# Second attention with stored values: one and three projection steps in turn, the output projection, the maxima and the next layernorm in other places

## The chip, the cores and the metric

One core of one Trainium2 chip. The metric is device microseconds of one execution; of several runs the median is told. Five engines work at once, each on its own queue in order: PE (TensorE matmuls; PEld is its weight load), DVE (VectorE), ACT (ScalarE), POOL (GpSimd) and SP (SyncE, which here issues nearly all DMA transfers). They wait for each other through semaphores.

## The reference

Four layers on a batch of 32 sequences of 128 tokens with 256 features, all in float32, each added to its input after a layernorm. The change touches the end of layer 2 and layer 3.

```python
x = x + _L0_xattn_ref(_layernorm(x), ctx_1024, ctx_1024, mask)      # 16 heads of 16, no weights
x = x + _L0_ffn_ref(_layernorm(x), w_gate, w_up, w_down)            # quantised, 256 -> 768 -> 256
x = x + _L1_xattn_ref(_layernorm(x), ctx_1024, ctx_1024, Wq, bq, ...)
x = x + _L1_ffn_ref(_layernorm(x), W1, b1, W2, b2, Wr, br)          # 8 experts, the best one per token

# _L1_xattn_ref: 16 heads of 64
q = query @ Wq + bq; k = key @ Wk + bk; v = value @ Wv + bv
attn = softmax(q k^T / 8)                                           # per head
out = (attn v) @ Wo + bo + residual
return (out - mean) * rsqrt(var + EPS) * ln_gamma + ln_beta
```

The quantised FFN rounds its activations with scales that are maxima over the whole batch, so its parts are separated by a global maximum each.

## The kernel before

The layers run one after the other. The order on PE, DVE, ACT and POOL is the order of the program text (`manual_schedule(engines=by_hand)`); SP is not in that set, and a planner places its transfers among each other.

**The FFN's last quantisation (about 465 to 543 us).** A loop over 16 half tiles (`order`, line 778 on) multiplies the quantised gate by the quantised up projection on ACT (L793, L796) and DVE (L799, L574). PE is free there, so the values of layer 3 are projected beside it: for 20 of the 32 sequences (`NF * G`) `project_v` multiplies the turned context tile `cf` by `wv_f` into PSUM (6 buffers), `take_v` copies the result to `vs` (5 buffers) on ACT or DVE, and SP stores it to `v_d` in DRAM. `load_v(b)` loads `cf` from DRAM; its pool `vf` has 2 buffers. Line 783 asks for the tile of block 4 + s once block 2 + s is projected. The first four halves (sequences 0 and 1) are projected in the stage before. When the loop is done, the global maximum `amax_o` gives `s_o` and `k_o` (L812 to L817), and the down projection begins with `quant_o` (L1195 on DVE, L1197 on ACT).

**The second attention (652 to 1290 us).** Two sequences are a group (`G`), 16 groups in all. A unit `n` is half the heads of one sequence `b`: 8 heads, `hf` is the half; a group has 4 units, `u` is the unit's place in it. Unit n does the following.

- `scores_c(n + 1)` on PE into the PSUM tiles `sc0` and `sc1` (one buffer each), `maxima(n + 1)` on DVE (L1012), `exps(n + 1, 0)` and `(n + 1, 1)` on ACT (L1021, 4 heads each, into `pr`, with sums), `normal_c(n + 1)`, which divides half on DVE and half on POOL (L1030, L1033).
- `transpose_c(n)` turns `pr` on PE into two `pt_p` tiles (2 buffers, shared with `pt_n`) and copies them to `prT` on ACT (L1048); `values_c(n)` multiplies by v (L1059) and copies to `oT` on ACT (L1066).
- Steps of the next group's projections: `step(g + 1, k)` for k = 0 to 7 computes 128 columns of K and of Q into one PSUM tile (L950; tag mm, 2 buffers), which its `take` copies to kT on ACT (L956) and to qT on DVE (L960). The rows of Q come from `rT`, the turned layernorm of the group.
- For an earlier sequence: `project_o` (L1072, 16 matmul instructions), `finish_1` to `finish_4` (sum, layernorm, residual, next layernorm, store of the row to `rows_d` by SP), `turn` and `logits` (PE, with the copy xnT on ACT), `route` (DVE: the best expert), `count` (PE, into the spare part of the `pt_n` tile) and `place` (DVE, then a scatter by POOL).
- For group g + 2: `norm_stats` (DVE, a power on POOL), `norm_apply` (DVE, two sums on POOL), `turn_group` and `turned_group` (PE, DVE: rT), and for group g + 3 `load_c` (three transfers on SP).

Where the next group's v comes from DRAM (`g + 1 < NF`, groups 0 to 8, 36 units) a unit has two steps: the short branch, which the change rewrites. Otherwise (28 units) three, since v has to be projected there; this branch is not rewritten.

Of the kernel before, what the change touches and what calls it, by code (L numbers as in the profile page):

```python
# [8 lines left out]
F32 = mybir.dt.float32  # L9
# [11 lines left out]
P = 128  # L21
# [15 lines left out]
def tile_xattn_ffn_d2(  # L37
# [27 lines left out]
    KD = D // P  # L65
# [588 lines left out]

    def load_v(b):
        if b < NF * G:
            cfs[b] = vf.tile([P, KD, P], F32, tag="cf", name="cf")
            nc.sync.dma_start(out=cfs[b], in_=ct_d[b])

    def project_v(b, h, ps):  # L660
# [9 lines left out]
        copy(vs, ps)  # L670
        nc.sync.dma_start(out=v_d[b, :, h * 512 : (h + 1) * 512], in_=vs)

    load_v(0)
    load_v(1)
    with (
        tc.tile_pool(name="bel", bufs=2, side="left") as el,
        tc.tile_pool(name="b_mu", bufs=6, space=PSUM) as pmm,
# [42 lines left out]
        for t in range(NT):  # L720
            up(t, 0)
            quant_g(t, 0)
            up(t, 1)
            sigmoid(t, 0)
            up(t, 2)
            if t % 2:
                b, h = divmod(t // 2, 2)
                ps_v = pv.tile([P, 512], F32, tag="v", name="ps_vf")
                project_v(b, h, ps_v)
                take_v(b, h, ps_v, el, nc.scalar.copy)  # L730
                if h:
                    load_v(b + 2)
            quant_s(t, 0)
            quant_g(t, 1)
            gate(t, 0)
            absmax("u", t, 0, ups[t, 0])
            up(t, 3)
            sigmoid(t, 1)
            up(t, 4)
            quant_s(t, 1)  # L740
            up(t, 5)
            if t < NT - 1:
                gate(t, 1)
            absmax("u", t, 1, ups[t, 1])
# [8 lines left out]
    with (  # L753
# [27 lines left out]
        for s, n in enumerate(order):  # L781
            took, taken = taken, []
            for h in range(2):
                taken.append(pv.tile([P, 512], F32, tag="v", name="ps_vf"))
                project_v(2 + s, h, taken[h])
            load_v(4 + s)
            if s >= KEPT:
                load_u(s + FU - 1)
            t, i = divmod(n, 2)
            r = half(gates[t], i)  # L790
            u = ups[t, i]
            u16 = ql.tile([P, HM, TB], I16, tag="u16", name="u16")
            nc.scalar.activation(u16, u, AF.Copy, scale=i_u)  # L793
            take(s, 0)
            gs16 = ql.tile([P, HM, TB], I16, tag="gs16", name="gs16")
            nc.scalar.activation(gs16, r, AF.Copy, scale=k_s)  # L796
            take(s, 1)

            nc.vector.scalar_tensor_tensor(r, gs16, s_s, u16, ALU.mult, ALU.mult)  # L799
            absmax("o", t, i, r)  # L800
# [296 lines left out]
    def finish_3(b):  # L1097
        t = tiles[b]
        t["ln"] = stats([t["row"][:, :D]], 1, "e")
# [228 lines left out]
    with tc.manual_schedule(engines=by_hand):  # L1328
        norm_stats(1)
        norm_apply(1)  # L1330
        values_of(0)
        for n in range(M1):
            step(0, n)()
# [10 lines left out]
        for n in range(N):  # L1344
            b, hf = divmod(n, 2)
            g, u = divmod(n, 2 * G)
            if u == 0 and g + 1 < NG:
                values_of(g + 1)
            nf = 2 if g + 1 < NF else 3
            fill = [  # L1350
                (lambda k=nf * u + j: step(g + 1, k)) if g + 1 < NG and j < nf
                else (lambda n=3 * (u if g + 1 == NG else -1) + j: others(n))
                for j in range(3)
            ]
            done = b - 2 if hf == 0 and b > 1 else None
            more = n + 1 < N
            if nf == 3:
                if more:
                    scores_c(n + 1)
                if u == 0 and g + 1 < NG and "rT" not in groups_[g + 1]:  # L1360
# [37 lines left out]
            else:  # L1398

                scores_c(n + 1)  # L1400
                maxima(n + 1)
                if hf and b > 0:
                    finish_1(b - 1)
                if u == 3:
                    norm_apply(g + 2)
                    load_c(g + 3)
                if done is not None:
                    finish_4(done)
                takes = [fill[0]()]
                exps(n + 1, 0)  # L1410
                transpose_c(n)
                takes.append(fill[1]())
                takes[0]()
                exps(n + 1, 1)
                takes[1]()
                if hf and b > 0:
                    finish_2(b - 1)
                values_c(n)
                if done is not None:
                    turn(done)  # L1420
                normal_c(n + 1)
                if u == 3:
                    turn_group(g + 2)
                    turned_group(g + 2)
                if hf and b > 0:
                    finish_3(b - 1)
                if hf == 0 and b > 0:
                    project_o(b - 1)
                if done is not None:
                    logits(done)  # L1430
                    if done > 0:
                        count(done - 1, tiles[done]["spare"])
                    route(done)
                    if done > 0:
                        place(done - 1)
            if u == 0 and g + 2 < NG:
                norm_stats(g + 2)
            if u == 2 and nf == 3 and g + 2 < NG:
                norm_apply(g + 2)
                if g + 3 < NG:  # L1440
                    load_c(g + 3)
            if u == 3 and nf == 3 and g + 2 < NG:
                turn_group(g + 2)
            if n == 8:
                first_weights()
# [301 lines left out]
```

## Time and profile before

| | us |
|---|---|
| median of 3 runs | 1617.8 (1615.79 to 1618.09) |
| the profiled execution | 1616.39 |
| its span | 1614.7 |
| values projected, last quantisation | 464.9 to 543.4 |
| down projection of the FFN | to 633.4 |
| short units of the second attention | 652.0 to 994.1 |
| its other units | 994.1 to 1290 |
| experts | 1330 to 1614.7 |
| PE busy in the span | 1521.8 |
| DVE / ACT / POOL busy | 950.5 / 809.0 / 461.1 |
| granted TensorE clock, mean | 0.988 |

The span runs from the first to the last instruction; the execution's time is 1.7 us longer. In a line of instructions in order of time stand the start, the length, the engine, the line of the program, the operation, output and inputs, the shape and the number of instructions that were merged; brackets tell how long the engine stood idle before it and who ended that. Matmul ends are modelled, so the distance from one start to the next tells more than the lengths.

### The profile page before, as it was taken

Reading aid. Unit: us, or ns where it says so; the run is one execution under the profiler, and the core shown is the slowest. Engines: PE = TensorE matmul, PEld = TensorE weight load, DVE = VectorE, ACT = ScalarE, POOL = GpSimd, SP = SyncE. Lnnn points to the kernel's source line nnn. Section 1 sums busy time; section 2 is a strip of 40 time slices with the busy share of each in tenths; the row PEclk is TensorE's granted clock in tenths of the full one; section 3 lists DMA queues with packets and bytes.
Section 4 is the critical chain, followed back from the end, with each engine's and each line's share of the span. In section 5 each row is a group of like instructions: output and inputs, shape, how many; then the busy total and the mean of one; then the engine's idle time right before and its main releaser. Section 6 shows DMA issues by size and latency. Waiting matters only on the chain. (4 is left out here: it accounts for less than half of the span.)

```text
span 1614.7 us, 28238 instructions
## 1 busy us (share of the span) xinstructions
PE 1521.8 (94%) x10062; PEld 1132.9 (70%) x10062; DVE 950.5 (59%) x2275; ACT 809.0 (50%) x2421; POOL 461.1 (29%) x533
## 2 busy tenths in 40 slices
PE   7999998999988899999999999999999969999997
PEld 4665665544433588787777777777777649999996
DVE  6989896347999434465555566566655433333332
ACT  5787885447979432655555555554455401111111
POOL 6566663000000002233333333323332222232321
PEclk9999999999999999999999999999999979999998
DMA  7222211002438756122111110010000343134410
GB/s 230 86 67 77 69 38 50 0 33 85 160 148 263 239 184 229 36 49 84 56 55 53 53 53 27 27 27 21 9 14 14 92 164 105 53 105 160 154 35 8
DMA packets 83724, 137.76 MB, mean 85 GB/s; under 512 B 13034, under 2 KB 61053, under 8 KB 80256
## 3 DMA queue, kind: packets, MB, share of 16 engines
q1 hardware_dynamic: 73664, 122.92, 23.0%
q0 software_dynamic: 5952, 12.61, 2.5%
q8 instruction: 80, 1.31, 0.4%
q10 hardware_dynamic: 3968, 0.42, 0.2%
q14 instruction: 60, 0.49, 0.1%
HBM read 159.48 MB, written 46.16 MB: 127 GB/s over the span
## 5 line engine op out<-in xcount | busy, mean ns | idle before, releaser
L1021 ACT ACTIVATE pr_c<-sc_c,nmaxc 128x128 f32<-128x128 f32 x512 | 183.4, 389 | 277.3 <-DVE nmaxc L1012 167.4
L1033 POOL TENSOR_TENSOR pr_c<-pr_c,rsumc 128x512 f32<-128x512 f32 x64 | 93.0, 1452 | 321.6 <-DVE rsumc L1030 181.5
L1642 ACT ACTIVATE hT<-h_ps,w1s 128x128 f32<-128x128 f32 x156 | 48.7, 364 | 254.0 <-issue 175.8
L960 DVE TENSOR_SCALAR qT<-ps_qk,bqk 128x256 f32<-128x256 f32 x128 | 61.8, 484 | 176.0 <-ACT kT L956 176.0
L1633 PEld LDWEIGHTS h_ps<-xbT,w1s 128*128 128x128 f32 x1248 | 147.5, 194 | 2.9 <-DVE xbT L1622 0.9
L1633 PE MATMUL h_ps<-xbT,w1s 128*128 128x128 f32 x1248 | 147.8, 277 | 0.5 <-DVE xbT L1622 0.5
L404 ACT ACTIVATE pr<-sc_a,nmaxa 128x128 f32<-128x128 f32 x512 | 139.9, 401 | 4.9 <-DVE nmaxa L395 4.9
L1657 PE MATMUL y_d<-w2s,hT 128*128 128x256 f32 x624 | 141.1, 379 | 0.0
L950 PE MATMUL ps_qk<-rT,wq_s 128*128 128x256 f32 x512 | 132.3, 381 | 7.0 <-DVE rT L934 7.0
L950 PE MATMUL ps_qk<-cT,wk_s 128*128 128x256 f32 x512 | 138.5, 393 | 0.0
L1657 PEld LDWEIGHTS y_d<-w2s,hT 128*128 128x128 f32 x624 | 115.5, 190 | 14.1
L1646 DVE TENSOR_SCALAR hT<-h_ps,w1s 128x128 f32<-128x128 f32 x156 | 47.5, 346 | 127.3 <-ACT hT L1642 125.3
L1072 PE MATMUL y_ps<-wo_s,oT 128*128 128x256 f32 x512 | 117.1, 382 | 0.0
L1021 ACT ACTIVATION_READ_ACCUMULATOR pr_c<-sc_c,nmaxc 128x1 f32 x512 | 116.7, 228 | 0.0
L950 PEld LDWEIGHTS ps_qk<-rT,wq_s 128*128 128x128 f32 x512 | 96.5, 190 | 23.3 <-DVE rT L934 10.6
L1072 PEld LDWEIGHTS y_ps<-wo_s,oT 128*128 128x128 f32 x512 | 94.7, 190 | 12.2 <-DVE pid L1496 0.4
L950 PEld LDWEIGHTS ps_qk<-cT,wk_s 128*128 128x128 f32 x512 | 87.5, 190 | 15.7 <-issue 2.1
L395 DVE TENSOR_REDUCE nmaxa<-sc_a 128x4 f32<-128x512 f32 x128 | 82.2, 684 | 16.0 <-PE sc_a L386 14.7
L1577 POOL DMA_INDIRECT xb<-rows_d,tok_i x39 | 39.9, 1023 | 178.2 <-PE y_d L1657 166.1
L1215 PE MATMUL ps_dn<-wdT,oq 128*128 128x256 f32 x384 | 83.7, 380 | 6.0 <-ACT oq L1197 6.0
L663 PE MATMUL ps_vf<-wv_f,cf 128*128 128x512 f32 x160 | 74.8, 620 | 12.4 <-DMA cf<-ct_d 10.6
L1215 PEld LDWEIGHTS ps_dn<-wdT,oq 128*128 128x128 f32 x384 | 72.7, 190 | 17.0 <-ACT oq L1197 7.2
(266 smaller groups left out, 3034.5 us busy)
## 6 DMA issues: line engine op xcount, KB each, us to landing
w1s<-in_W1b_dram SPq DMA_DIRECT2D x39, 1028.0 KB
w2s<-in_W_dram SPq DMA_DIRECT2D x39, 1024.0 KB
v_d<-vs SPq DMA_DIRECT2D x40, 256.0 KB
v<-v_d SPq DMA_DIRECT2D x10, 1024.0 KB
u_d<-u SPq DMA_DIRECT2D x12, 768.0 KB
ub<-u_d SPq DMA_DIRECT2D x12, 768.0 KB
w2e<-in_W_dram SPq DMA_DIRECT2D x8, 1024.0 KB
rows_d<-row SPq DMA_DIRECT2D x32, 256.0 KB
```

Source lines behind the costliest of these rows:

```text
L395: nc.vector.tensor_reduce(u["nmax"][:, r, :], u["scs"][r], AX.X, ALU.max, negate=True)
L404: nc.scalar.activation(u["pr"][:, r * HQ + j, :], u["scs"][r][:, j, :], AF.Exp, bias=u["nmax"][:, r, j : j + 1],)
L663: nc.tensor.matmul(ps, lhsT=cfs[b][:, k, :], rhs=wv_f[:, k, h * 512 : (h + 1) * 512], start=(k == 0), stop=(k == KD - 1),)
L950: nc.tensor.matmul(ps[:, j, :], lhsT=w_[:, k, m * P : (m + 1) * P], rhs=src[:, k, :], start=(k == 0), stop=(k == KD - 1),)
L960: nc.vector.tensor_scalar(s["qT"][:, m, :], ps[:, 1, :], bqk[:, 0, m : m + 1], HD1**-0.5, ALU.add, ALU.mult,)
L1021: nc.scalar.activation(u["pr"][:, h, :], u["scs"][par][:, mm, :], AF.Exp, bias=u["nmax"][par][:, mm : mm + 1], accum_out=u["sums"][:, h : ...
L1033: eng.tensor_tensor(pr[:, j : j + 4, :], pr[:, j : j + 4, :], bc(rsum[:, j : j + 4], 2, P), ALU.mult,)
L1072: nc.tensor.matmul(t["y_ps"][:, :D], lhsT=t["oT"][:, m, :], rhs=wo_s[:, m, :], start=(m == 0), stop=(m == M1 - 1),)
L1215: nc.tensor.matmul(ps[:, j, :], lhsT=oq[:, m, j * P : (j + 1) * P], rhs=wdT[:, m, :], start=(m == 0), stop=(m == M0 - 1),)
L1633: nc.tensor.matmul(h_ps[:, c4, :], lhsT=wb[:, k * FF + c * P : k * FF + (c + 1) * P], rhs=xbT[:, k, :], start=(k == 0), stop=(k == KD - 1),)
L1642: nc.scalar.activation(hT[:, c, :], h_ps[:, c4, :], AF.Relu, bias=b1c)
L1657: nc.tensor.matmul(y_ps[:, :D], lhsT=hT[:, c, :], rhs=w2t[:, c, :], start=(c == 0), stop=(c == MF - 1),)
```

## The change

`cf` gets three buffers, and every load is asked for one block further ahead. In the short branch:

- the steps are 1 in the first half (`hf` 0) and 3 in the second, in place of 2 and 2; the third one comes behind the values;
- in the first half `project_o(b - 1)` and `turn` stand ahead of the values, not behind them;
- `place` moves from the end of the first half, where it stood ahead of the next unit's maxima, to behind these maxima in the second half;
- `norm_apply(g + 2)`, `load_c(g + 3)`, `turn_group` and `turned_group` move from u = 3 to u = 1, `norm_stats(g + 2)` from behind unit u = 0 to its middle.

```diff
@@ -654,7 +654,7 @@
 
     def load_v(b):
         if b < NF * G:
-            cfs[b] = vf.tile([P, KD, P], F32, tag="cf", name="cf")
+            cfs[b] = vf.tile([P, KD, P], F32, tag="cf", name="cf", bufs=3)
             nc.sync.dma_start(out=cfs[b], in_=ct_d[b])
 
     def project_v(b, h, ps):
@@ -670,8 +670,8 @@
         copy(vs, ps)
         nc.sync.dma_start(out=v_d[b, :, h * 512 : (h + 1) * 512], in_=vs)
 
-    load_v(0)
-    load_v(1)
+    for b in range(3):
+        load_v(b)
     with (
         tc.tile_pool(name="bel", bufs=2, side="left") as el,
         tc.tile_pool(name="b_mu", bufs=6, space=PSUM) as pmm,
@@ -729,7 +729,7 @@
                 project_v(b, h, ps_v)
                 take_v(b, h, ps_v, el, nc.scalar.copy)
                 if h:
-                    load_v(b + 2)
+                    load_v(b + 3)
             quant_s(t, 0)
             quant_g(t, 1)
             gate(t, 0)
@@ -783,7 +783,7 @@
             for h in range(2):
                 taken.append(pv.tile([P, 512], F32, tag="v", name="ps_vf"))
                 project_v(2 + s, h, taken[h])
-            load_v(4 + s)
+            load_v(5 + s)
             if s >= KEPT:
                 load_u(s + FU - 1)
             t, i = divmod(n, 2)
@@ -1328,6 +1328,7 @@
     with tc.manual_schedule(engines=by_hand):
         norm_stats(1)
         norm_apply(1)
+        placing = []
         values_of(0)
         for n in range(M1):
             step(0, n)()
@@ -1346,15 +1347,21 @@
             g, u = divmod(n, 2 * G)
             if u == 0 and g + 1 < NG:
                 values_of(g + 1)
-            nf = 2 if g + 1 < NF else 3
-            fill = [
-                (lambda k=nf * u + j: step(g + 1, k)) if g + 1 < NG and j < nf
-                else (lambda n=3 * (u if g + 1 == NG else -1) + j: others(n))
-                for j in range(3)
-            ]
+
+
+            short = g + 1 < NF
+            if short:
+                steps = range(4 * (u // 2) + hf, 4 * (u // 2) + (4 if hf else 1))
+                fill = [(lambda k=k: step(g + 1, k)) for k in steps]
+            else:
+                fill = [
+                    (lambda k=3 * u + j: step(g + 1, k)) if g + 1 < NG
+                    else (lambda n=3 * u + j: others(n))
+                    for j in range(3)
+                ]
             done = b - 2 if hf == 0 and b > 1 else None
             more = n + 1 < N
-            if nf == 3:
+            if not short:
                 if more:
                     scores_c(n + 1)
                 if u == 0 and g + 1 < NG and "rT" not in groups_[g + 1]:
@@ -1399,47 +1406,54 @@
 
                 scores_c(n + 1)
                 maxima(n + 1)
+                if hf and placing:
+                    place(placing.pop())
                 if hf and b > 0:
                     finish_1(b - 1)
-                if u == 3:
+                if done is not None:
+                    finish_4(done)
+                if u == 0:
+                    norm_stats(g + 2)
+                if u == 1:
                     norm_apply(g + 2)
                     load_c(g + 3)
-                if done is not None:
-                    finish_4(done)
-                takes = [fill[0]()]
+                take = fill[0]()
                 exps(n + 1, 0)
                 transpose_c(n)
-                takes.append(fill[1]())
-                takes[0]()
+                take()
                 exps(n + 1, 1)
-                takes[1]()
-                if hf and b > 0:
-                    finish_2(b - 1)
+                if hf:
+                    take = fill[1]()
+                    take()
+                    if b > 0:
+                        finish_2(b - 1)
+                else:
+                    if b > 0:
+                        project_o(b - 1)
+                    if done is not None:
+                        turn(done)
                 values_c(n)
-                if done is not None:
-                    turn(done)
                 normal_c(n + 1)
-                if u == 3:
-                    turn_group(g + 2)
-                    turned_group(g + 2)
-                if hf and b > 0:
-                    finish_3(b - 1)
-                if hf == 0 and b > 0:
-                    project_o(b - 1)
+                if hf:
+                    fill[2]()()
+                    if b > 0:
+                        finish_3(b - 1)
+                    if u == 1:
+                        turn_group(g + 2)
+                        turned_group(g + 2)
                 if done is not None:
                     logits(done)
                     if done > 0:
                         count(done - 1, tiles[done]["spare"])
+                        placing.append(done - 1)
                     route(done)
-                    if done > 0:
-                        place(done - 1)
-            if u == 0 and g + 2 < NG:
+            if u == 0 and not short and g + 2 < NG:
                 norm_stats(g + 2)
-            if u == 2 and nf == 3 and g + 2 < NG:
+            if u == 2 and not short and g + 2 < NG:
                 norm_apply(g + 2)
                 if g + 3 < NG:
                     load_c(g + 3)
-            if u == 3 and nf == 3 and g + 2 < NG:
+            if u == 3 and not short and g + 2 < NG:
                 turn_group(g + 2)
             if n == 8:
                 first_weights()
```

## Prediction

> **What bounds the kernel now.** I read the page first (busy shares, then the slices), then busy times by stretch for the two stages that the diff touches, then the instructions of each engine in order of time inside them. Columns of the second and later lines: stretch, its length, busy time (instructions) of PE, PEld, DVE, ACT, POOL, granted clock, DMA share, GB/s.
>
> ```profile
> PE 1521.8 (94%) x10062; PEld 1132.9 (70%) x10062; DVE 950.5 (59%) x2275; ACT 809.0 (50%) x2421; POOL 461.1 (29%) x533
> ...
> 651.97:994.07 342.10, 325.63 (x2451) 270.60 (x2451) 200.72 (x620) 187.00 (x772) 113.86 (x110) 1.00 0.17 51
> 464.94:543.40 78.46, 67.27 (x144) 27.80 (x144) 69.80 (x58) 61.10 (x60) 1.05 (x3) 0.96 0.77 261
> 994.07:1290.00 295.93, 292.73 (x2000) 221.58 (x2000) 174.08 (x527) 144.79 (x580) 87.65 (x89) 1.00 0.10 28
> ```
>
> 651.97 to 994.07 are the 36 short units; 994.07 on are units that the diff leaves alone, on a PE with 3 us idle. So a microsecond saved among the short units is a microsecond of the kernel if it is a wait of PE. Where PE waits is seen in one group of four units (start, length, instruction, in brackets the idle before it and who ended it):
>
> ```profile
> 721.42 1.16 PE L1002 MATMUL sc_c<-kT,qT 64*128 64x128 f32 x16
> 722.51 1.13 PE L950 MATMUL ps_qk<-cT,wk_s 128*128 128x256 f32 x4
> 724.47 1.13 PE L950 MATMUL ps_qk<-rT,wq_s 128*128 128x256 f32 x4 [0.83 <-DVE rT L934]
> ...
> 740.45 0.48 PE L1002 MATMUL sc_c<-kT,qT 64*128 64x128 f32 x2
> 741.63 1.16 PE L1002 MATMUL sc_c<-kT,qT 64*128 64x128 f32 x14 [0.70 <-ACT pr_c L1021]
> 742.72 1.13 PE L950 MATMUL ps_qk<-cT,wk_s 128*128 128x256 f32 x4
> ```
>
> The reader is to see two waits per group. The projection waits for rT (724.47 less 722.51 is 1.96 where 0.97 is usual: 0.99 lost). The scores wait for the exponentials that still read the only PSUM pair (742.72 less 740.45 is 2.27 where 1.09 is usual: 1.18 lost). Smaller ones in the same group are 0.38 and 0.2 for prT and 0.29 for POOL's half of pr. Together 3.1 of a period of 38.83 (721.42 to 760.25).
>
> The second stage is the value projection under the FFN's last quantisation:
>
> ```profile
> 516.69 12.23 PE L663 MATMUL ps_vf<-wv_f,cf 128*128 128x512 f32 x24 [2.33 <-DMA cf<-ct_d]
> ...
> 528.36 0.69 DVE L670 COPY vs<-ps_vf 128x512 f32<-128x512 f32 x1 [2.91 <-DMA v_d<-vs]
> ...
> 541.44 0.16 DVE L817 TENSOR_TENSOR k_o<-i_o,s_u 128x1 f32<-128x1 f32 x1
> ...
> 543.39 1.95 DVE L1195 TENSOR_SCALAR o<-r,k_o 128x1536 int16<-128x1536 f32 x2 [1.79 <-PE ps_vf L663]
> ```
>
> PE waits 10.6 us in five places for cf, DVE once for a vs buffer, and the next stage starts when PE's last block is done, 1.8 after its factor k_o is.
>
> **The third cf buffer.** It adds no instruction: a load is issued when block s has been read, as now, but for block s+3, so it has 3.44 us more (8 matmuls of 0.43, a block). A load lands 2.3 after issue (issued 514.39, PE went on at 516.69), so PE's waits go. Then DVE sets the pace: two iterations take 7.62 (483.69 to 491.31), ACT's 7.30, PE's 6.9. DVE's 2.91 idle is a chain: store of vs behind a cf load on SP's queue, that load behind PE, PE behind the cf load before. It goes too, so k_o is ready at 541.6 - 2.9 = 538.7. PE's last half block needs the PSUM buffer that DVE's copy at 535.99 frees, now 533.1 + 0.7; with 2.0 of matmuls it ends near 536. The quantisation starts at 538.7 instead of 543.4: **4.6**. If DVE still waits for its buffer only the 1.8 come; SP now issues eleven stores in a row at the end, ahead of the x1 loads, which are needed 8 us later, so I bound a new wait at -1. Range -1 to 5. The projection stage behind is continuous on PE from 559.94 and only moves.
>
> **The short units, PE.** Sum of start-to-start steps that show no wait: scores 1.09; a step 1.83; transposes 0.87; values 1.03; output projection 3.46; pt_n 0.27; logits 0.36; counts 0.12. The one-step unit is 9.05. For the three-step unit a row exists, since the untouched units have the same order of matmuls:
>
> ```profile
> 1009.23 1.16 PE L1002 MATMUL sc_c<-kT,qT 64*128 64x128 f32 x16
> ...
> 1016.84 1.03 PE L950 MATMUL ps_qk<-rT,wq_s 128*128 128x256 f32 x4
> 1017.80 1.16 PE L1002 MATMUL sc_c<-kT,qT 64*128 64x128 f32 x16
> ```
>
> 8.57. With turn_group (0.58) a group is 2 x 9.05 + 2 x 8.57 + 0.58 = 35.8 if nothing waits. No matmul is added or removed; what is won is waits.
>
> How much wait there is, two rules read differently. PE's busy row has 342.1 - 325.6 = 16.5 idle in the short units. The Trainium skill, "Perfetto Trace Analysis", section "Identifying the Most-Contended Engine", says that matmul busy share is a poor measure of headroom as matmuls are pipelined, and to take the share of weight loading: 270.6 of 342.1, 79%, leaving 71 us. By the first the stage can't gain over 16.5, by the second 71 is thinkable. I take neither but the start-to-start sums: the wait of 1.18 above is booked as only 0.70 idle, while back-to-back matmuls with their weight loads in between leave PEld at 79% with nothing to gain.
>
> **Do the other engines keep up?** Three-step unit, 0 = start of its scores, durations from the rows of 760 to 785. DVE: route 0.2 to 1.2 (it waits for the counts, the matmuls just before); maxima 1.28, to 2.5; place, now behind them, 0.73, to 3.2; finish_1 1.2, to 4.4; in u = 1 norm_apply 0.73, to 5.1; qT 0.48 when ACT's kT is done; qT again 6.7 to 7.2; finish_2 0.96; reciprocal and its half of pr 0.9, to 9.0; third qT; finish_3 0.74, to 10.3; in u = 1 rT 0.6, to 10.9. ACT: exponentials 2.0 to 3.3, two prT copies to 4.5, kT to 4.9, exponentials to 6.2, kT 6.7, oT 7.5, kT. POOL: place's scatter 1.06 (ahead of rsd, which is first needed at 7.2), in u = 1 the two sums of 1.26 (to 7.8), pr 1.45 from 8.2, pow. So the exponentials are done 2.4 before the next scores (8.57): the 1.18 wait goes. prT is there 1 us before its values: the 0.4 go. rT is ready two units ahead: the 0.99 go. place must read its counts before the second half of the transposes, which reuses that PSUM buffer: 2.9 against 3.36, so moving it behind the maxima is free, and costs what it is late beyond that. finish_1 frees y_ps's buffer at 3.6, values need it at 5.6: the sooner output projection is free too.
>
> One-step unit: DVE arrives 1.9 into it, 0.7 after the scores; exponentials to 4.1, prT 5.1, kT 5.5, exponentials 6.8; PE needs prT at 7.6, the scores' PSUM at 9.05. pt_n at 7.3 needs the row of finish_4 (3.6); ACT's xnT, now ahead of oT on its queue, is ready at 8.3, logits come at 8.6; oT follows at 8.8 and is first read 13 us later. norm_stats (1.28, u = 0) ends at 4.9, before qT at 5.5. All hidden. The moved steps bring with them 5 DVE instructions and a pow (norm_stats), 2 and 2 sums on POOL (norm_apply), four transposes and a DVE copy (turn_group), and on SP load_c's three transfers, which stand one group ahead of use, behind the row store of an earlier tile; x2 is read a group (36 us) after its issue.
>
> **A new wait.** The last step of a group (m = 7) is now issued at the very end of the three-step unit u = 3, and the scores right behind need it. kT and qT of one PSUM tile are taken one after the other:
>
> ```profile
> 778.50 0.52 ACT L956 ACTIVATE kT<-ps_qk,bqk 128x256 f32<-128x256 f32 x1
> ...
> 779.05 0.48 DVE L960 TENSOR_SCALAR qT<-ps_qk,bqk 128x256 f32<-128x256 f32 x1 [1.17 <-ACT kT L956]
> ```
>
> PE's results are readable 0.17 after 8.57; kT 0.54, qT 0.5: 9.8. The scores of m = 7 are the last quarter of 1.09 and would start at 8.57 + 0.82 = 9.4. PE stands 0.4 to 0.5, with everything of the next unit behind it; I take 0.47, once per group. If DVE is late there it is more (to 1.2), without it 0.
>
> **Sum.** Group: 35.8 + 0.47 = 36.3, against 38.83: 2.5, in seven groups (721.42 to 994.07) 17.8. Group 1 has one count less: 36.2 against 37.56, 1.4. Group 0: unit 0 has no output projection and its chain of exponentials sets it, 6.4; then 9.15, 8.3, 8.57: 32.4 against 31.9, a loss of 0.5. Unit 36 keeps its form but loses the 0.99 and gets the 0.47: 0.5. Together 19.2, with the first stage **23.8**. The profiled execution took 1616.4 (span 1614.7 and 1.7 around it), so 1592.6; the median of the runs is 1.4 above it, so **1594.0**.
>
> **Rivals.** (a) The waits of the units don't go wholly: something takes 0.3 to 0.6 per pair (the place reads, xnT's 0.3 of slack). For it: DVE has about 9.6 us of work in a three-step unit of 9.1. Against: slack in the one-step unit. Gain 13 to 18: 1599 to 1605. (b) The loads were hidden anyway and DVE keeps its buffer wait: 19.2 + 1.8: 1597. (c) m = 7 costs nothing and group 0 nothing: 1589. (d) Slower: DVE becomes the bound of a pair. Its work behind the maxima spills into the one-step unit; from a start of the maxima 4.1 in (computed 1.9), exponentials end after 9.05 and each microsecond more is one per pair. Eighteen pairs: 23.8 are gone at 1.3 more, when maxima start 5.4 in. For it: "DVE qT waits for ACT kT" is the longest DVE wait of the stage. Against: DVE is busy 201 of 342, and these waits are in the working. At 6 in it is 1628.
>
> **Chances.** As summed, with small errors of its terms: 0.55 (1590 to 1598); (a) 0.17, (b) 0.10, (c) 0.12, (d) 0.06. Range: 1586 to 1605, which takes in (a), (b) and most of (c). Of (d) 0.05 end slower. A measurement of this kernel tells some 0.2%, 3 us. Faster 0.93, same 0.02, slower 0.05.
>
> **What would show it.** Right: unit periods of 9.0 and 8.6 to 9.2, no wait for rT, waits of the scores on qT of about 0.5 every fourth unit, no PE wait for cf, the quantisation L1195 near 538.7. Wrong: PE waiting for place or route in the transposes, DVE waiting for x2, vs stores still holding DVE.

## The result, and the profile after

The changed kernel takes **1590.65 us** (median of five runs, 1586.6 to 1592.86) against 1617.97 (1615.79 to 1619.16) for the kernel before on the same chip: ratio 0.9828, 95% interval 0.9809 to 0.9848, or 27.3 us. The prediction was 1594.0 in a range of 1586 to 1605. The profiled execution of the changed kernel took 1592.86 us with a span of 1591.2.

First the page's busy row of the changed kernel.

```profile
PE 1517.2 (95%) x10062; PEld 1134.3 (71%) x10062; DVE 953.8 (60%) x2275; ACT 819.8 (52%) x2421; POOL 461.3 (29%) x533
```

The number of instructions of every engine is the one of before: nothing was taken out, only moved. Now the busy times by stretch (stretch, length, then PE, PEld, DVE, ACT, POOL, granted clock, DMA share, GB/s) for the value projection and the 36 short units.

```profile
467.95:541.73 73.78, 64.24 (x144) 26.50 (x144) 69.69 (x58) 61.22 (x60) 1.05 (x3) 1.00 0.81 281
648.72:972.34 323.62, 320.95 (x2451) 271.10 (x2451) 205.66 (x625) 197.07 (x771) 114.42 (x111) 1.00 0.24 54
```

78.45 has become 73.77, 342.10 has become 323.62. PE's idle time in the short units went from 16.5 us to 2.7 with the same 2451 matmuls. One group of four units follows, PE in order of time (start, length, instruction, in brackets the idle before it).

```profile
699.73 1.16 PE L1002 MATMUL sc_c<-kT,qT 64*128 64x128 f32 x16
700.82 1.13 PE L950 MATMUL ps_qk<-cT,wk_s 128*128 128x256 f32 x4
701.78 1.03 PE L950 MATMUL ps_qk<-rT,wq_s 128*128 128x256 f32 x4
...
708.90 1.16 PE L1002 MATMUL sc_c<-kT,qT 64*128 64x128 f32 x16
...
717.47 0.94 PE L1002 MATMUL sc_c<-kT,qT 64*128 64x128 f32 x12
718.62 0.49 PE L1002 MATMUL sc_c<-kT,qT 64*128 64x128 f32 x4 [0.21 <-DVE qT L960]
719.04 1.13 PE L950 MATMUL ps_qk<-cT,wk_s 128*128 128x256 f32 x4
...
727.13 1.16 PE L1002 MATMUL sc_c<-kT,qT 64*128 64x128 f32 x16
...
736.13 1.16 PE L1002 MATMUL sc_c<-kT,qT 64*128 64x128 f32 x16
```

From scores to scores the units take 9.17, 8.57, 9.66 and 9.00, 36.40 a group where 38.83 stood. The projection follows its scores at once (700.82 to 701.78 is the usual 0.96), so the wait for rT is gone. The scores are whole in three units of four. In the fourth the last four matmuls wait for the qT of the last step: 717.47 to 719.04 is 1.57 where 1.09 is usual, 0.48 lost.

In the value stage, in order of time:

```profile
523.79 14.04 PE L663 MATMUL ps_vf<-wv_f,cf 128*128 128x512 f32 x32 [0.65 <-DMA cf<-ct_d]
...
541.44 0.16 DVE L817 TENSOR_TENSOR k_o<-i_o,s_u 128x1 f32<-128x1 f32 x1
541.72 1.95 DVE L1195 TENSOR_SCALAR o<-r,k_o 128x1536 int16<-128x1536 f32 x2
```

PE waits for cf once, 0.65, where it waited 10.6 in all before, and the quantisation follows its factor at once, where it stood 1.79 for PE before.

The stages, each from the first PE instruction of its kind to the next stage's (the value stage to L1195):

| stage | before | after | saved |
|---|---|---|---|
| value projection to L1195 | 78.45 | 73.77 | 4.68 |
| first ps_dn to the first short unit's scores | 105.89 | 104.32 | 1.57 |
| 36 short units | 342.10 | 323.62 | 18.48 |
| the unit behind them | 15.16 | 13.28 | 1.88 |

The sum is 26.6. The spans differ by 23.5, since in this one execution of the changed kernel the stages ahead of all edits ended 3.0 later (the value stage began at 467.95 instead of 464.94). Runs of one kernel differ by as much, so stage lengths are the sharper measure here, and they are used below.

### The profile page after: what moved, and what is told of

It is laid out like the page before. It is cut to its first block, busy times and chain, and to the rows that moved or that the text cites. A ratio compares the mean times of both kernels' runs of the same rounds, so it can differ in the third digit from the quotient of the medians.

```text
span 1591.2 us, 28202 instructions
## 1 busy us (share of the span) xinstructions
PE 1517.2 (95%) x10062; PEld 1134.3 (71%) x10062; DVE 953.8 (60%) x2275; ACT 819.8 (52%) x2421; POOL 461.3 (29%) x533
## 5 line engine op out<-in xcount | busy, mean ns | idle before, releaser
L956 ACT ACTIVATE kT<-ps_qk,bqk 128x256 f32<-128x256 f32 x128 | 63.6, 498 | 57.4 <-PE ps_qk L950 57.4
L395 DVE TENSOR_REDUCE nmaxa<-sc_a 128x4 f32<-128x512 f32 x128 | 82.3, 685 | 16.5 <-PE sc_a L386 15.3
L1215 PEld LDWEIGHTS ps_dn<-wdT,oq 128*128 128x128 f32 x384 | 74.2, 194 | 17.8 <-ACT oq L1197 7.4
```

What stands on the lines that cost most here:

```text
L395: nc.vector.tensor_reduce(u["nmax"][:, r, :], u["scs"][r], AX.X, ALU.max, negate=True)
L956: nc.scalar.activation(s["kT"][:, m, :], ps[:, 0, :], AF.Identity, bias=bqk[:, 1, m : m + 1])
L1215: nc.tensor.matmul(ps[:, j, :], lhsT=oq[:, m, j * P : (j + 1) * P], rhs=wdT[:, m, :], start=(m == 0), stop=(m == M0 - 1),)
```

## The experiments

Two theories were set against each other. **A**, as the prediction reads: the three-step unit is long enough for the exponentials, the early layernorm takes the wait for rT, the other moves are free and gain nothing. **B**, formed when the trace of after was read: the exponentials were late in the kernel before because place and norm_stats stand ahead of the maxima on DVE. So the order on DVE is what pays, the parts are substitutes or covers for each other, and the split may cost more than it brings.

All runs in one table. "Value" and "units" are the first and third stage above; "group" is a steady group of four units. The times are medians, the ratio is to the kernel before on the same chip (1618.0 for after, 1619.3 to 1619.9 for the others), with its 95% interval. Stage lengths come from one profiled execution each.

| kernel | us | ratio | value | units | group |
|---|---|---|---|---|---|
| before | | | 78.45 | 342.10 | 38.83 |
| after | 1590.65 | 0.9828 (0.9809-0.9848) | 73.77 | 323.62 | 36.41 |
| e1 cf3 | 1611.66 | 0.9954 (0.9940-0.9969) | 73.75 | 341.89 | 38.87 |
| e2 attention alone | 1597.09 | 0.9860 (0.9840-0.9880) | 78.84 | 324.82 | 36.41 |
| e3 two and two | 1588.20 | 0.9811 (0.9792-0.9831) | 73.77 | 316.84 | 35.78 |
| e4 norm late | 1589.36 | 0.9818 (0.9797-0.9838) | 73.75 | 321.47 | 36.09 |
| e5 turn late | 1587.08 | 0.9805 (0.9789-0.9822) | 73.76 | 320.53 | 36.02 |
| e6 maxima first alone | 1600.20 | 0.9894 (0.9871-0.9916) | 76.66 | 326.43 | 36.77 |
| e7 split alone | 1622.75 | 1.0022 (1.0012-1.0033) | 77.85 | 349.25 | 39.44 |
| e8 place back | 1592.30 | 0.9839 (0.9818-0.9860) | 73.77 | 326.45 | 36.77 |
| e9 norm early alone | 1618.03 | 0.9984 (0.9974-0.9995) | 78.82 | 339.70 | 38.63 |
| e10 projection late | 1602.70 | 0.9902 (0.9882-0.9921) | 73.76 | 334.18 | 37.63 |
| e11 two and two, projection late | 1591.50 | 0.9832 (0.9817-0.9846) | 73.75 | 323.08 | 36.57 |
| e12 late maxima | 1592.42 | 0.9840 (0.9819-0.9861) | 73.75 | 324.76 | 36.41 |

**The two stages apart.** e1 is the kernel before with the third buffer alone:

```diff
-            cfs[b] = vf.tile([P, KD, P], F32, tag="cf", name="cf")
+            cfs[b] = vf.tile([P, KD, P], F32, tag="cf", name="cf", bufs=3)
-    load_v(0)
-    load_v(1)
+    for b in range(3):
+        load_v(b)
-                    load_v(b + 2)
+                    load_v(b + 3)
-            load_v(4 + s)
+            load_v(5 + s)
```

> The kernel before with the third cf buffer alone (loads three blocks ahead); the attention is left as before. Theory: the wait for cf was PE's, the wait for the vs buffer followed from it, so both go: first block of the value projection to the quantisation L1195 takes 73.8 us instead of 78.45, PE waits under 1 us for cf, the short units stay at 342.1. Time 4.6 less than before (1613.4), and 1.6 more if the down projection's start gains as well, as the trace of after has it. Rival (loads hidden anyway, DVE keeps its buffer wait): 76.6 for the stage, 1.8 less.

e2 is the changed kernel with these lines as in before.

> The changed kernel with two cf buffers as before, so the attention part of the change alone. Theory (the two parts are independent, since PE only shifts in between): value stage 78.45 as before, short units 323.6 and unit 36 at 13.3 as in after, 19 to 21 less than before, 1597 to 1599. Rival (the attention part loses part of its gain when it begins later, or the two share a cause): short units at 328 or more.

Waits of PE in the value stage of e1 (engine, tile and line, who is waited for; us in total, times, longest):

```profile
PE ps_vf L663 <- ACT vs L670: 2.9, 2, 2.5
...
PE ps_vf L663 <- DMA cf<-ct_d: 1.2, 1, 1.2
```

By the times e1 gains 5 to 10 us (the interval of its ratio) and e2 22.8 (19.4 to 25.9), against 4.6 or 6.2 and 19 to 21 expected. The value stage takes 73.75 in e1 and 78.84 in e2, the short units 341.89 and 324.82: the parts don't touch each other, as the theory has it. (e2's units are 1.2 longer than after's because its first unit began at a granted clock of 0.66, between 651.19 and 656.26, where after had 1.00; the same stands at the start of e6's units, 0.67. One wait for cf of 1.2 is more than the "under 1 us" expected.) All nine kernels with three buffers have 73.75 to 73.77, all five with two have 76.66 to 78.84.

The granted clock changes with the buffers too: over this stage it is 0.93 to 0.98 in the five kernels with two and 1.00 in the nine with three, and PE's busy time for the same 144 matmuls went from 67.27 to 64.24. That both come with the third buffer is shown by e1; how much of the 4.7 us is the waits and how much the clock, no run separates.

e1 also gains 1.78 in the down projection (105.89 to 104.11), which the prediction did not have. In order of time, of e2, which has two buffers (ACTq is ACT's queue issuing a transfer):

```profile
544.21 1.95 DVE L1195 TENSOR_SCALAR o<-r,k_o 128x1536 int16<-128x1536 f32 x2 [1.80 <-PE ps_vf L663]
...
549.52 3.61 ACTq L843 DMA_DIRECT2D bvT<-in_L_xattn_bv_dram  x1
...
553.17 3.39 ACTq L848 DMA_DIRECT2D row_bo<-in_L_xattn_bo_dram  x1
...
558.11 3.04 ACT L1197 ACTIVATE oq<-o,s_o 128x1536 f32<-128x1536 int16 x2 [9.80 <-DMA row_bo<-in_L_xattn_bo_dram]
...
559.74 3.50 PE L1215 MATMUL ps_dn<-wdT,oq 128*128 128x256 f32 x15 [2.22 <-ACT oq L1197]
```

And of e1, with three:

```profile
539.89 1.95 DVE L1195 TENSOR_SCALAR o<-r,k_o 128x1536 int16<-128x1536 f32 x2
...
543.98 4.69 ACTq L843 DMA_DIRECT2D bvT<-in_L_xattn_bv_dram  x1
548.71 1.35 ACTq L848 DMA_DIRECT2D row_bo<-in_L_xattn_bo_dram  x1
...
551.61 1.57 ACT L1197 ACTIVATE oq<-o,s_o 128x1536 f32<-128x1536 int16 x1 [7.62 <-DVE o L1195]
```

ACT issues loads of parameters between two blocks of oq. In e2 the last long issue ends 12.4 after the quantisation began (553.17 + 3.39 - 544.21), oq is late and PE stands 2.22. In e1 it ends 10.2 after (548.71 + 1.35 - 539.89), and oq waits for nothing but its input. The idle for oq is there in all five kernels with two buffers (1.78 to 3.24) and in none of the nine with three. That it goes with the third buffer is shown; why the issues begin sooner then, and bvT and row_bo together take less (6.0 against 7.0), is not.

Of the 3.24 that stood in the kernel before only 1.6 is won. The rest goes to the clock at the start of the down projection, first before, then after (columns as above):

```profile
546.08:551.68 5.60, 5.60 (x26) 4.95 (x27) 1.11 (x2) 1.41 (x1) 0.20 (x1) 1.00 0.58 167
544.40:550.00 5.60, 5.60 (x17) 4.65 (x18) 1.00 (x1) 1.41 (x1) 0.00 (x0) 0.65 0.90 304
```

PE is done with the values earlier and stands 6.57 ahead of the down projection, 2.72 in the kernel before. The granted clock is then 0.65 in the first 5.6 us, where it was 1.00, and the first 40 matmuls take 10.66 instead of 8.74.

**The order on DVE.** e6 is the kernel before with place behind the maxima and norm_stats in the middle of a unit:

```diff
                 scores_c(n + 1)
                 maxima(n + 1)
+                if hf and placing:
+                    place(placing.pop())
                 if hf and b > 0:
                     finish_1(b - 1)
...
                 if done is not None:
                     finish_4(done)
+                if u == 0:
+                    norm_stats(g + 2)
...
                         count(done - 1, tiles[done]["spare"])
+                        placing.append(done - 1)
                     route(done)
-                    if done > 0:
-                        place(done - 1)
-            if u == 0 and g + 2 < NG:
+            if u == 0 and nf == 3 and g + 2 < NG:
                 norm_stats(g + 2)
```

> The kernel before, with one part alone: place goes behind the maxima of the next unit and norm_stats into the middle of a unit; two steps per unit, output projection, norm_apply and cf buffers as before. Theory B (order on DVE made the exponentials late): the wait of the scores for pr goes, the period of 12.58 becomes 11.4 or less and the 11.95 stays for want of rT, group 38.83 to 37.3 or 37.7, 9 to 12 us less than before. Theory A (only a longer unit gives the exponentials their time): 12.58 stays, time as before.

The kernel before, around the scores of unit 1, in order of time:

```profile
733.37 1.16 PE L1002 MATMUL sc_c<-kT,qT 64*128 64x128 f32 x16
...
734.56 0.16 DVE L1154 TENSOR_TENSOR at<-pt_n,free 128x8 f32<-128x8 f32 x1
...
735.29 0.42 DVE L895 BATCH_NORM_STATS2 stc<-x2c 128x6 f32<-128x256 f32 x1
...
736.56 1.28 DVE L1012 TENSOR_REDUCE nmaxc<-sc_c 128x4 f32<-128x512 f32 x2
...
741.31 0.27 ACT L1021 ACTIVATION_READ_ACCUMULATOR pr_c<-sc_c,nmaxc 128x1 f32 x1
```

The same place in e6:

```profile
730.84 1.16 PE L1002 MATMUL sc_c<-kT,qT 64*128 64x128 f32 x16
...
732.03 1.29 DVE L1012 TENSOR_REDUCE nmaxc<-sc_c 128x4 f32<-128x512 f32 x2
...
737.01 0.24 ACT L1021 ACTIVATION_READ_ACCUMULATOR pr_c<-sc_c,nmaxc 128x1 f32 x1
737.48 0.71 PE L1002 MATMUL sc_c<-kT,qT 64*128 64x128 f32 x8
```

In before the maxima start 3.19 after the scores (736.56 - 733.37), since place (from 734.56, 0.73) and norm_stats (from 735.29, 1.27) stand ahead of them; the last exponential ends 8.2 after the scores' start, in a unit of 7.08. In e6 the maxima start at 1.19, the exponentials end 6.4 after the scores' start, 0.2 ahead of the next scores, in a unit of only 6.64. So a two-step unit is long enough. The group is 36.77: the order alone gives 2.06, where the whole change gives 2.42. The units are 15.7 shorter, more than the 9 to 12 us expected. Theory A, that the exponentials need a longer unit, falls. What place and norm_stats are worth apart no run shows: in the kernel before, the other unit of a group with place ahead of its maxima, the one at 753.02, is 7.23 long and the scores behind it don't wait.

**The split.** e7 is the kernel before with one and three steps alone:

```diff
+            if nf == 2:
+                steps = range(4 * (u // 2) + hf, 4 * (u // 2) + (4 if hf else 1))
+                fill = [(lambda k=k: step(g + 1, k)) for k in steps]
...
-                takes.append(fill[1]())
+                if hf:
+                    takes.append(fill[1]())
...
-                takes[1]()
+                if hf:
+                    takes[1]()
...
                 normal_c(n + 1)
+                if hf:
+                    fill[2]()()
```

> The kernel before, with the split into one and three steps alone; place and norm_stats ahead of the maxima, output projection behind the values, norm_apply in the last unit, two cf buffers. Theory B: a one-step unit with the output projection behind its values has only 1.09 + 1.83 + 0.87 = 3.8 of PE ahead of values whose prT is ready at 5.1, so each one-step unit waits 1.3 us and more; what the scores and rT gain is given back: group between 38 and 39.5, time within 8 us of before. Theory A (the split is what removes the waits): group at 36.4 to 37, 15 to 20 us less than before.

e3 is the changed kernel without the split:

```diff
-                steps = range(4 * (u // 2) + hf, 4 * (u // 2) + (4 if hf else 1))
+                steps = range(2 * u, 2 * u + 2)
...
+                take = fill[1]()
+                take()
                 if hf:
-                    take = fill[1]()
-                    take()
                     if b > 0:
                         finish_2(b - 1)
...
                 if hf:
-                    fill[2]()()
                     if b > 0:
                         finish_3(b - 1)
```

> The changed kernel with two projection steps in every short unit, the rest of the change (maxima ahead of place, sooner output projection, norm two units sooner, third cf buffer) kept. Theory A, as the prediction reads (the split gives the exponentials their time): the 1.18 wait of the scores in the two-step unit comes back, one per two units, 7 to 21 us more than after. Theory B (formed from the trace of after): in before the exponentials were late because place 0.73 and norm_stats 1.28 stood ahead of the maxima on DVE, so with maxima first the exponentials end near 6.2 of a unit of 6.7 and nothing waits; and the last step now stands before the values, so the scores of m = 7 no longer wait for their qT: 0.5 per group, 4 us less than after, short units near 319.5.

PE in e7, the scores behind a three-step unit and the values of the one-step unit that follows:

```profile
745.24 1.16 PE L1002 MATMUL sc_c<-kT,qT 64*128 64x128 f32 x16
746.33 1.13 PE L950 MATMUL ps_qk<-cT,wk_s 128*128 128x256 f32 x4
...
750.69 1.15 PE L1059 MATMUL o_c<-prT_c,v 128*64 128x128 f32 x16 [1.50 <-ACT prT_c L1048]
```

PE in e3:

```profile
722.98 1.16 PE L1002 MATMUL sc_c<-kT,qT 64*128 64x128 f32 x16
...
730.21 1.16 PE L1002 MATMUL sc_c<-kT,qT 64*128 64x128 f32 x16
...
741.11 1.16 PE L1002 MATMUL sc_c<-kT,qT 64*128 64x128 f32 x16
...
747.75 1.19 PE L1002 MATMUL sc_c<-kT,qT 64*128 64x128 f32 x16
```

The split alone costs 0.61 per group: with the output projection behind the values, a one-step unit has too little PE work ahead of them, and they wait for prT, 1.50 at the worst. The wait that it was to remove does go: the scores behind the three-step unit take the usual 1.09 (745.24 to 746.33). So a longer unit is one way to get the exponentials done in time and the order on DVE is another, but the longer unit is paid for in the values. Taken out of the changed kernel, the units become 7.23, 10.90, 6.64 and 11.01, a group of 35.78, and no scores wait. That is the sum of steps without waits that the prediction gave as 35.8. So in a steady group the split brings nothing that the rest does not bring, and costs 0.63: the 0.48 of m = 7, and 0.15 in small steps (a one-step unit is 9.18 where the sum has 9.05). Over the 36 units e3 is 6.8 us shorter than after. The unit behind them takes 14.67 instead of 13.28, for there PE stands 1.61 for prT and in after not at all, so 5.4 are left. The intervals of the two times overlap and don't tell them apart.

**The early layernorm.** e9 is the kernel before with norm_apply and turn_group in unit 1, alone:

```diff
-                if u == 3:
+                if u == 1:
                     norm_apply(g + 2)
                     load_c(g + 3)
...
-                if u == 3:
+                if u == 1:
                     turn_group(g + 2)
                     turned_group(g + 2)
```

> The kernel before, with norm_apply, its loads and turn_group in unit 1 instead of unit 3, alone. Theory: the wait of 0.83 idle (0.99 of period) for rT goes from eight groups, 11.95 becomes 10.96, the other waits stay: 38.83 to 37.9, 8 us less than before. Rival (norm_apply's 0.73 of DVE now stands in the unit whose scores already wait for the exponentials): 12.58 grows by up to 0.7, and 2 to 3 us are left of the 8.

e4 makes the reverse edit in the changed kernel, and e5 moves turn_group and turned_group alone back to u == 3.

> The changed kernel with norm_apply, its loads and turn_group put back to the last unit of a group, as before. Theory A: the early layernorm is what took the 0.99 wait for rT, so it comes back once per group: 8 to 9 us more than after, less the 0.48 of m = 7 that goes (turn_group's 0.58 of transposes stands between the last step and the scores again): 4 to 5 more in sum. Theory B (with 1/3 the group ends 2.1 later behind norm_apply's start than with 2/2, rT is ready at 10.97 and read at 11.2): no wait for rT, none for m = 7: 4 us less than after.

> The changed kernel with turn_group alone put back into the last unit of a group, behind the third step (norm_apply stays two units sooner). Theory: its 0.58 of transposes is work that does not need qT, standing between the last step and the scores that do, so the wait of m = 7 shrinks from 0.48 to 0.1 or less without any other change: group 36.0, short units 3 to 4 us less than in after. Rival (the wait is DVE's lateness and moves on, as with place put back): no difference, 36.4.

PE's waits in e9, between 645 and 972, and in order of time around the scores of unit 0:

```profile
PE o_c L1059 <- ACT prT_c L1048: 7.0, 13, 0.7
...
756.34 1.16 PE L1002 MATMUL sc_c<-kT,qT 64*128 64x128 f32 x16
...
762.98 1.72 PE L1002 MATMUL sc_c<-kT,qT 64*128 64x128 f32 x16
764.63 1.13 PE L950 MATMUL ps_qk<-cT,wk_s 128*128 128x256 f32 x4
```

PE in e4, from a group's last step to the next unit's projection:

```profile
712.39 1.03 PE L950 MATMUL ps_qk<-rT,wq_s 128*128 128x256 f32 x4
713.25 0.60 PE L925 MATMUL pt_c<-ident,r 128*128 128x128 f32 x4
713.78 1.56 PE L1002 MATMUL sc_c<-kT,qT 64*128 64x128 f32 x16
715.27 1.13 PE L950 MATMUL ps_qk<-cT,wk_s 128*128 128x256 f32 x4
716.24 1.08 PE L950 MATMUL ps_qk<-rT,wq_s 128*128 128x256 f32 x4
```

In e9 no wait for rT is left among PE's waits, yet a group gains only 0.20, the units 2.4 in all: unit 0 goes from 11.95 to 11.74 instead of 10.96. The move also takes turn_group's 0.59 of transposes out of unit 3, the one at 756.34, which goes from 7.23 to 6.64. They had stood ahead of unit 0's scores; now these lose 0.56 (762.98 to 764.63 is 1.65 where 1.09 is usual), with place still ahead of the maxima, and the values 0.2 for prT. (The rival said so for the wrong unit: 12.58 did not grow, it went to 12.28, and unit 1 grew, by the transposes and a wait of its values.) In e4 no wait for rT comes back (715.27 to 716.24 is 0.97), for a unit with a third step is longer behind norm_apply by that step, 1.83. Both late placings make the changed kernel's group shorter: 36.09 and 36.02 instead of 36.41, because turn_group's transposes stand between the last step and the scores that need its qT. e5 saves 3.1 in the units, as expected. e4 saves 2.15 there, about half of the 4 expected, since in some units the scores still take 0.1 to 0.4 longer (713.78 to 715.27 above is 1.49). The times of both overlap with after's and don't tell them apart.

**The moves called free.** e10 puts the output projection behind the values again, e8 puts place ahead of the maxima again, e11 makes e10's edit in e3:

```diff
-                    if b > 0:
-                        project_o(b - 1)
-                    if done is not None:
-                        turn(done)
                 values_c(n)
+                if done is not None:
+                    turn(done)
                 normal_c(n + 1)
...
+                if hf == 0 and b > 0:
+                    project_o(b - 1)
```

> The changed kernel with the output projection and pt_n put back behind the values of the one-step unit, all else as in after. Theory: the projection's 3.46 of PE is what covers the exponentials of a one-step unit; without it values wait for prT from 3.8 to 5.1, 1.3 us per pair and 2.6 a group: one-step units of 10.4, short units 20 to 24 us longer than in after. Rival (the place of the projection is free, since DVE and ACT keep up anyway): no difference.

> Two steps per unit (as in the run with two steps everywhere and the rest of the change) but with the output projection and pt_n behind the values again. Theory: with two steps ahead of the values prT is nearly there, and the projection covers what the run with maxima first alone still showed, 11.22 against 10.90: 0.3 per even unit, group 35.78 to 36.4, 5 us more than with the projection sooner. Rival: nothing, the gain of the sooner projection belongs to the one-step units alone.

```diff
-                if hf and placing:
-                    place(placing.pop())
...
-                        placing.append(done - 1)
                     route(done)
+                    if done > 0:
+                        place(done - 1)
```

> The changed kernel with place put back ahead of the maxima (end of the one-step unit, behind route), all else as in after. Theory (slack of the three-step unit covers it: exponentials end at 6.2 + 0.73 of 8.57, prT has 1 us and keeps 0.3): short units as in after, 36.4 a group, no difference in time. Rival (the order on DVE is what pays here too): 0.3 to 0.73 per pair, 5 to 12 us more than after.

e10's waits of PE, between 645 and 972:

```profile
PE o_c L1059 <- ACT prT_c L1048: 9.3, 18, 1.1
```

e8, the end of a group's last unit, PE and DVE in order of time:

```profile
711.93 0.94 PE L1002 MATMUL sc_c<-kT,qT 64*128 64x128 f32 x12
...
712.30 0.69 DVE L1033 TENSOR_TENSOR pr_c<-pr_c,rsumc 128x512 f32<-128x512 f32 x1
712.91 0.48 DVE L960 TENSOR_SCALAR qT<-ps_qk,bqk 128x256 f32<-128x256 f32 x1
...
713.44 0.49 PE L1002 MATMUL sc_c<-kT,qT 64*128 64x128 f32 x4 [0.57 <-DVE qT L960]
```

The place of the projection is worth 1.22 per group with the split (expected: 2.6), 10.6 us over the 36 units, half of the 20 to 24 expected. The expectation had prT ready at 5.1; in e10 the values start 4.7 to 4.8 after the scores, and in unit 0 half a microsecond of their wait is already spent on m = 7. With two steps per unit it is worth 0.79 (36.57 to 35.78), so the rival there, that only one-step units need it, falls too. Place ahead of the maxima costs 0.36 per group, and not through the exponentials' PSUM: everything behind the maxima is later, and last on DVE's queue stands the qT of m = 7 behind finish_2 and the reciprocal. What these scores lose grows from 0.48 to 0.84 (711.93 to the projection behind them, 713.87, is 1.94 where 1.09 is usual).

**Slack of the one-step unit.** e12 computes the maxima twice in every one-step unit, 1.28 more on DVE ahead of the exponentials:

```diff
                 scores_c(n + 1)
+                if not hf:
+                    for par in range(2):
+                        again = small.tile([P, 4], F32, tag="again", name="again")
+                        nc.vector.tensor_reduce(
+                            again, units[n + 1]["scs"][par], AX.X, ALU.max, negate=True
+                        )
                 maxima(n + 1)
```

> The changed kernel with the maxima computed twice in every one-step unit (1.28 us more of DVE ahead of the exponentials, its result unused), to measure the slack that the prediction counts on there. Theory: exponentials end at 8.1 of 9.05 and prT is there at 6.4 of 7.6, so no difference, short units 323 to 325. Rival (DVE is the bound of a pair): 1.28 per pair, 22 us more than after.

The group stays at 36.41. The units are 1.14 longer, of which 1.0 is in group 0, whose unit 0 has no output projection:

```profile
650.46 1.15 PE L1059 MATMUL o_c<-prT_c,v 128*64 128x128 f32 x16 [1.25 <-ACT prT_c L1048]
```

So the slack is there, up to the 1.28 tried, and where the projection is missing so is the slack.

## Why the prediction was right, and where it was not

**The whole.** The time is 3.4 us, 0.2%, below the forecast. The sum of steps was 23.8; the stages saved 26.6. The 2.8 between them are 1.6 of the down projection and 1.4 of the unit behind the short ones, less 0.2 of the short units. The time alone says little for the reasons: e3, e4, e5, e8, e11 and e12, which undo or add parts, take 1587 to 1592 and lie in the range of the forecast as well.

**Third cf buffer: right.** 4.6 predicted, 4.68 measured, and 4.70 by e1. PE's waits for cf and DVE's 2.91 went together, so the chain was read rightly, and rival (b), 1.8, falls. k_o was ready at 541.60, 73.65 into the stage; predicted was 538.7 - 464.94 = 73.76. The clock, 0.96 in this stage in the kernel before, was not in the working, and its part stays open.

**"The projection stage behind is continuous on PE from 559.94 and only moves": wrong by 1.6.** The sentence starts at 559.94, and the idle of 3.24 that ends there, for oq behind ACT's loads, was left out of the reckoning. So was the lower clock at the stage's start, which takes about half of it back.

**Unit periods: right.** Predicted 9.05, 8.57, 9.05 plus 0.47, and turn_group's 0.58; measured 9.18, 8.57, 9.66 and 9.00, the last with turn_group in it. Group 36.3 against 36.41; group 0 32.4 against 32.39, group 1 36.2 against 36.36. That the seven groups saved just the 17.8 forecast is partly luck: each came out 0.12 longer than forecast, and in the kernel before they were 38.95 on average, not 38.83 as the one group read, again 0.12. The two rules of the prediction's middle part gave 16.5 and 71 as limits; 18.5 was gained, so PE's idle row alone would have been too low by 2, and the start-to-start sums were right. In e3, where PE is busy for all of the 316.84, weight loading still takes only 271.0 of them, 86%: its idle share was not headroom here. (The waits that the prediction lists for one group add up to 3.04, not 3.1.)

**m = 7: right.** 0.47 predicted, 0.48 measured, nine times. e5 takes it away but for 0.1 by moving 0.58 of unrelated transposes in between. Rival (c), where it costs nothing, falls, though its time (1589) lies nearer to the result than the forecast's.

**"So the exponentials are done 2.4 before the next scores (8.57): the 1.18 wait goes": true, but the longer unit was not needed for it.** They are done 6.4 into the unit, 2.2 before. The order on DVE is enough: e6 ends its exponentials at 6.4 too, in a unit of 6.64. "Moving it behind the maxima is free" stands in the prediction as a price of nothing with no gain beside it; with norm_stats it carries 2.06 of 2.42 per group.

**"rT is ready two units ahead: the 0.99 go": true of the wait, not of the time.** Alone the move brings 0.20 (e9), for waits on the exponentials and on prT come up. In the split loop rT is in time with norm_apply late (e4), so its part there is nothing.

**"The sooner output projection is free too": wrong as a part.** It is the cover of the one-step unit: 1.22 a group (e10), and 0.79 with two steps everywhere (e11).

**Unit 36, 0.5 predicted, 1.88 measured.** The 1.11 that pt_n waited there for prT in the kernel before goes too; the sum left it out. It is the split that takes it away: with two steps (e3) it is 1.61.

**(a) and (d).** Neither came about. (d)'s mechanism was tried up to 1.28 of delay in the one-step units and cost nothing in steady groups (e12); its break-even at 5.4 was not tried. e8 shows DVE's lateness being paid in the last unit of a group, at half its size.

What each part does to a steady group, one after the other, by the runs:

| step | group | difference |
|---|---|---|
| before | 38.83 | |
| maxima first (e6) | 36.77 | -2.06 |
| norm two units sooner, third cf buffer (e11) | 36.57 | -0.20 |
| output projection sooner (e3) | 35.78 | -0.79 |
| split into one and three (after) | 36.41 | +0.63 |

The forecast was right because it summed the finished loop, stage by stage, instead of adding up gains of parts. Its reasons for each wait were not tested by that sum, and of three of them (the longer unit, the early layernorm, the sooner projection) the worth was not what it said.

## What to carry to other kernels

Forecast a reordered loop as a whole, from start-to-start steps and the time at which each producer is done; a part's own worth depends on which other waits lie behind the one that it removes, and only undoing it shows that. Before lengthening a stage to cover a late producer, look at what stands ahead of that producer on its own queue: moving 2.0 us of unrelated work behind the maxima did more (36.77 a group) than giving the exponentials a longer unit (39.44). When the last producer of a loop body feeds the first consumer of the next, put work between them that needs neither (0.6 us of transposes took away all but 0.1 of a wait of 0.48).

## What was not expected of the hardware

The value stage takes 73.75 to 73.77 us in nine kernels with three cf buffers, and 76.66, 77.85, 78.45, 78.82 and 78.84 in the five with two: with the loads off PE's path, a spread of 2.2 us between the profiled executions went as well. The granted clock fell to 0.67 between 485 and 490 us and to 0.74 between 515 and 520 in the kernel before and stayed at 1.00 there in the changed one, which lost 1.9 us to a clock of 0.65 at the start of the down projection instead. The low stretches came behind waits of PE (3.88, 2.33 and 6.57), but not behind every wait: the 2.69 ahead of the first short unit was followed by 1.00 in after and by 0.66 in e2. And an issue of a small parameter load on ACT's queue took between 0.4 and 4.9 us in these traces (wr_s 0.44, bvT 4.89 in e3), long enough for the next block of oq to be late behind it; where the time goes within such an issue no run here tells.
